# First attention's rotation sums, sums of squares, power and query planes moved from the projection into a stage of their own behind the scores

## The chip, the core and the metric

The kernel runs on one core of one Trainium2 chip. The time is the device time of one launch in microseconds; a version's figure is the median of several runs. Engines are named as the profile names them: PE (TensorE matmuls), PEld (TensorE weight loads), DVE (VectorE), ACT (ScalarE), POOL (GpSimd), SP (SyncE, which issues the DMAs).

## What is computed

Two transformer layers, each attention and then a feed-forward part, on an input of 4 sequences x 256 positions x 256 features in f32. Only the first attention is touched. Per sequence, with 16 query heads, 8 key/value heads and head size 128:

```python
q = einsum('btd,ndh->btnh', x, q_kernel);  k, v = einsum('bsd,ckdh->cbskh', x, kv_kernel)
q = apply_rope(rms_norm(q, q_norm_scale)); k = apply_rope(rms_norm(k, k_norm_scale))
mask = (j <= i) & (i - j < 128)
probs = softmax(where(mask, (q * ATTN_SCALE) @ k, min))
x = x + einsum('btnh,nhd->btd', probs @ v, out_kernel)        # x was layer-normed before q, k, v
```

The first feed-forward part (with a 2-of-4 sparsification), the second attention and the second feed-forward part (with a Hadamard transform) follow.

## The kernel before, in words

The first attention is a software pipeline (`pipelined`, L301) over 16 units: n = 4b+g is sequence b with head group g (4 query heads, 2 key/value heads). Six stages are called with lags 0, 1, 2, 3, 4, 4 in steps. In one step the code calls them in the order project, join, split, score, turn, attend, each for its own unit. A scheduler in the language's layer then orders the instructions of each engine from this; `tc.issue_after(x)` holds an instruction behind x in that order. Every engine runs its queue in the order it was given.

- **project** (`project0`, L409): for both row halves t, PE multiplies the normed x by the q weights (4 heads) and the k,v weights (L426, tiles pj). DVE multiplies each result by the sine and the cosine table (L431, tiles qs and qc), ACT squares it (L436, sq) and copies v out (L438). Then, still in project: DVE adds the two rotated parts (L443, the *rotation sum*, 128x768) and reduces the squares per head (L444, the *sum of squares*, ss). For n >= 6 POOL splits the queries into two 16-bit planes (L242 through `copy_gpsimd`, tile qpl), which SP transposes by DMA (L454, qplT). POOL then makes the inverse root by a power (L457, L460, L463, tile r) and scales the keys with it (L466).
- **turn** (`turn0`, L472), one step later: queries come to qT from the DMA's planes (DVE, L486), or for n < 6 through PE transposes (L481) and a DVE copy (L482); keys go through PE transposes (L492, tr_k) and an ACT copy to kT (L493).
- **score** (`probabilities`, L192), two steps behind project: four score tiles on PE (L204, L205), for each two masked copies with row maxima on DVE (L207, mx), the bias on DVE (L214, nb), exponentials on ACT (L217), reciprocals on DVE (L222, rs), normalization on POOL (L225).
- **split, join, attend**: POOL splits p into planes (L242, tile pl), SP transposes them (L251, plT), ACT joins them (L262, pT), PE multiplies with v (L380, L384, tile av), ACT copies av out (L388, zT). In the last units PE transposes p instead.
- **out** (L391): behind steps 8, 9, 12 and 13 one block of the output projection (L294, tile po).

PSUM has eight banks here: four of the tag `bank` (scores, av, po, early tr_k) and four of the tag `half` (pj, tr_q, and tr_k for 6 <= n < 14). A tile's bank is free for the next tile of its tag when its readers are done: scores by L207 on DVE, pj by L431 on DVE with L436 and L438 on ACT, av by ACT. The squares have two buffers, one for each t.

Of the kernel before, what the change touches and what calls it, by code (L numbers as in the profile page):

```python
# [20 lines left out]
F32 = mybir.dt.float32  # L21
# [3 lines left out]
ALU = mybir.AluOpType  # L25
AX = mybir.AxisListType

P = 128
B, T, D = 4, 256, 256
NT = T // P  # L30
# [18 lines left out]
def two_layers(ctx, tc, consts, tables, x, wq, wkv, wo, w_gate, w_up, w_down,  # L49
               w_k, w_q, w_v, w_o, w1, w3, w2, out):  # L50
    nc = tc.nc
# [92 lines left out]
    last_of = {}  # L144
# [171 lines left out]
    def attention0():  # L316
        with tc.tile_pool(name="attn0", bufs=2, reuse_waits="tile", side="right") as own:
            xnT, factors = {0: normed(0)}, {}


            cos_s = own.tile([P, NT, 2, HD], F32, name="cos_s", bufs=1)
            sin_s = own.tile([P, NT, 2, HD], F32, name="sin_s", bufs=1)
            with tc.issue_after(last_of["norm"].ins):
                for t in range(NT):
                    for tab, at in ((cos_s, 0), (sin_s, 256)):
                        src = angles[:, at + t * HD : at + (t + 1) * HD]
                        nc.vector.tensor_tensor(
                            tab[:, t], src.unsqueeze(1).to_broadcast([P, 2, HD]), scl, ALU.mult
                        )

            def project(n, _):
                b, g = divmod(n, 4)
                held = project0(own, xnT[b], g, cos_s, sin_s, n >= 6)
                if g == 1 and b + 1 < B:
                    factors[b + 1] = moments(b + 1)
                if g == 2 and b + 1 < B:
                    with tc.issue_after(last_of["qc"].ins):
                        xnT[b + 1] = normed(b + 1, factors[b + 1])
                return held

            def turn(n, held):
                rot, qT_planes, v, r = held
                return *turn0(own, rot, qT_planes, half if 6 <= n < 14 else bank), v, r

            def score(n, held):
                qT, kT, v, r = held
                ps = [
                    probabilities(
                        qT, kT, (2 * kk, 2 * kk + 1), mask0,
                        r[:, :, 2 * kk : 2 * kk + 2].rearrange("p t h -> p h t"),  # L350
                    )
                    for kk in range(2)
                ]
                return ps, v

            def split(n, held):
                ps, v = held
                return ps if n >= B * 4 - 3 else [
                    planes(p, own_planes) for p in ps
                ], v  # L360

            def own_planes(shape, name):
                return own.tile(shape, U16, tag="pl", name=name, bufs=4)

            def join(n, held):
                ps, v = held
                return [
                    transposed(ps[kk]) if n >= B * 4 - 3 else joined(ps[kk], ((
                        (nc.scalar.copy, slice(0, 2), last_of["exp"]),
                        (nc.scalar.copy, slice(0, 2), last_of["exp"]),  # L370
                    )[kk],)) for kk in range(2)
                ], v

            def attend(n, held):
                pTs, v = held
                zT = page("zT")
                for kk in range(2):
                    pT = pTs[kk]
                    av = bank([2, T], "av")
                    nc.tensor.matmul(  # L380
                        av, lhsT=v[:, 0, kk, :], rhs=pT[:, :, 0:T], start=True, stop=False,
                        skip_group_check=True,
                    )
                    nc.tensor.matmul(  # L384
                        av[:, :, P:T], lhsT=v[:, 1, kk, :], rhs=pT[:, :, T:],
                        start=False, stop=True, skip_group_check=True,
                    )
                    nc.scalar.copy(zT[:, 2 * kk : 2 * kk + 2, :], av)  # L388
                return zT

            def out(b, t, kept=False):  # L391
                def emit(done):
                    zTs = [done[4 * b + g] for g in range(4)]
                    if not kept:
                        project_out(bank([D], "po"), zTs, wo_sb, b, t)
                    else:
                        with tc.issue_after(last_of[0].ins):
                            project_out(half([D], "po"), zTs, wo_sb, b, t)
                return emit

            behind = {
                8: [out(0, 0)], 9: [out(0, 1)], 12: [out(1, 0)], 13: [out(1, 1)],
                17: [lambda _: xn_f.append(normed(0))],
                19: [lambda _: xn_f.append(normed(1)),
                     out(2, 0, True), out(2, 1, True), out(3, 0), out(3, 1)],
            }
            pipelined((project, turn, score, split, join, attend), (0, 1, 2, 3, 4, 4), behind, (0, 4, 3, 2, 1, 5))

    def project0(own, xnT, g, cos_s, sin_s, by_dma):  # L409


        v = own.tile([P, NT, 2, HD], F32, tag="v", name="v", bufs=5)
        r = small.tile([P, NT, 6], F32, tag="r", name="r")
        ss = small.tile([P, NT, 6], F32, tag="ss", name="ss")
        rot = []
        for t in range(NT):
            cols = slice(t * P, (t + 1) * P)
            sq = own.tile([P, 6, HD], F32, tag="sq", name="sq", bufs=2)
            qc = own.tile([P, 6, HD], F32, tag="qc", name="qc", bufs=4)
            qs = own.tile([P, 6, HD], F32, tag="qs", name="qs")  # L420

            for w, hs in ((wq_sb, slice(0, 4)), (wkv_sb, slice(4, 6))):
                pj = half([4, HD], "pj")
                n = hs.stop - hs.start
                for c in range(NC):
                    last_of[0] = nc.tensor.matmul(  # L426
                        pj, lhsT=xnT[:, c, cols], rhs=w[:, g, c, :],
                        start=(c == 0), stop=(c == NC - 1),
                    )
                for rot_to, tab in ((qs, sin_s), (qc, cos_s)):  # L430
                    last_of["qc"] = nc.vector.tensor_tensor(  # L431
                        rot_to[:, hs], pj[:, 0:n],
                        tab[:, t, hs.start // 4, :].unsqueeze(1).to_broadcast([P, n, HD]),
                        ALU.mult,
                    )
                nc.scalar.activation(sq[:, hs], pj[:, 0:n], AF.Square)  # L436
                if n == 2:
                    last_of["v", t] = nc.scalar.copy(v[:, t, :, :], pj[:, 2:4])  # L438
            rot.append((qc, qs, sq))
        for t, (qc, qs, sq) in enumerate(rot):  # L440

            parts = [i.rearrange("p n (s h) -> p n s h", s=2) for i in (qc, qs)]
            nc.vector.tensor_tensor(parts[0], parts[0], parts[1][:, :, ::-1, :], ALU.add)  # L443
            nc.vector.tensor_reduce(ss[:, t, :], sq, AX.X, ALU.add)  # L444
            rot[t] = qc
        qT_planes = None
        if by_dma:

            planes = page_of_planes([P, NT, 2, 4 * HD], "qpl")
            for t, qc in enumerate(rot):  # L450
                words = qc[:, 0:4, :].rearrange("p j h -> p (j h)").bitcast(U16)
                copy_gpsimd(planes[:, t], words.rearrange("p (n w) -> p w n", w=2))
            qT_planes = page_of_planes([P, NT * 2 * 4, P], "qplT")
            nc.sync.dma_start_transpose(qT_planes, planes.rearrange("p t w n -> p (t w n)"))  # L454

        ve = small.tile([P, NT, 6], F32, tag="ve", name="ve")
        nc.gpsimd.tensor_scalar(  # L457
            ve[:, :, 0:4], ss[:, :, 0:4], 1.0, HD * RMS_EPS, ALU.mult, ALU.add
        )
        nc.gpsimd.tensor_scalar(  # L460
            ve[:, :, 4:6], ss[:, :, 4:6], 1.0 / HD, RMS_EPS, ALU.mult, ALU.add
        )
        nc.gpsimd.tensor_tensor(r.rearrange("p t h -> p (t h)"), ve.rearrange("p t h -> p (t h)"),  # L463
                                mhalf, ALU.pow)
        for t, qc in enumerate(rot):
            last_of["k"] = nc.gpsimd.tensor_tensor(  # L466
                qc[:, 4:6, :], qc[:, 4:6, :],
                r[:, t, 4:6].unsqueeze(2).to_broadcast([P, 2, HD]), ALU.mult,
            )
        return rot, qT_planes, v, r  # L470

    def turn0(own, rot, qT_planes, bank_of_k):  # L472

# [474 lines left out]
```

## Time and profile before

| | |
|---|---|
| median of 3 runs | 755.07 us (754.88 to 755.31) |
| the profiled execution | 755.64 us, its span 753.8 us |
| granted TensorE clock | 1.000 |
| first attention | about 7 to 265 us of the span |
| busy, whole span | PE 98%, DVE 61%, ACT 53%, POOL 44% |

The profile is of one execution. An engine's busy time is the union of its instructions. Ends of matmuls are modelled, and each has a tail behind the time in which the next may start; so stalls of PE are best read from start to start: 0.430 us between two matmuls of 512 columns, 0.215 for 256, 0.109 for 128 when nothing is waited for.

### The profile page before, as it was taken

To read this page: it belongs to the slowest core of one execution; us is meant where nothing else is said; L and a number is where in the kernel's file an instruction comes from. 1 tells how busy PE (TensorE), PEld (TensorE's weight loads), DVE (VectorE), ACT (ScalarE), POOL (GpSimd) and SP (SyncE) were. 2 spreads that over 40 slices of the span, in tenths; PEclk is the share of its full clock that TensorE was granted. 3 is DMA by queue.
4 is the path that set the end of the run, shared out by engine and by line. 5 is a ranking of instruction groups with operands and counts; after the bars stand their busy time and mean duration, and the time that the engine had idled before them with its cause. 6 is when DMAs were issued, how large, how long until landed. Compare 5 with 4: busy or idle time off the path is not lost. (4 is left out here: it accounts for less than half of the span.)

```text
span 753.8 us, 11642 instructions
## 1 busy us (share of the span) xinstructions
PE 738.6 (98%) x3980; PEld 601.4 (80%) x3980; DVE 462.1 (61%) x1396; ACT 399.7 (53%) x985; POOL 330.0 (44%) x475
## 2 busy tenths in 40 slices
PE   8999999999999999999999999999999999999998
PEld 5556556656666788888899999999998899899997
DVE  6999886698678426987655644464443447344433
ACT  2378886678668722222346555555555675415332
POOL 1589998779678301011116433343338644220000
PEclk9999999999999999999999999999999999999999
DMA  8725445435433060001334422432232222002100
GB/s 322 284 42 71 69 86 100 82 59 108 73 70 71 1 223 14 16 15 22 119 70 84 127 43 43 98 100 43 43 71 43 43 43 42 2 0 22 27 10 28
DMA packets 121610, 53.30 MB, mean 71 GB/s; under 512 B 114768, under 2 KB 116944, under 8 KB 120784
## 3 DMA queue, kind: packets, MB, share of 16 engines
q1 hardware_dynamic: 121552, 52.57, 30.6%
q8 instruction: 31, 0.51, 0.3%
q14 instruction: 27, 0.22, 0.1%
HBM read 22.94 MB, written 1.05 MB: 32 GB/s over the span
## 5 line engine op out<-in xcount | busy, mean ns | idle before, releaser
L225 POOL TENSOR_SCALAR p<-p,rs 128x128 f32<-128x128 f32 (+1 forms) x256 | 120.9, 491 | 156.7 <-DVE rs L222 153.4
L207 DVE CUSTOM_DVE_ANT_0 p<-sc,cst 128x128 f32<-128x128 f32 (+1 forms) x256 | 78.7, 350 | 10.4 <-PE sc L205 7.8
L242 POOL TENSOR_SCALAR pl<-p 128x1536 uint16<-128x1536 uint16 x54 | 81.9, 1516 | 6.3 <-DMA plT<-pl 2.1
L262 ACT COPY pT<-plT 128x768 uint16<-128x768 uint16 (+1 forms) x54 | 77.1, 1486 | 1.8 <-DMA plT<-pl 1.8
L217 ACT ACTIVATE p<-p,nb,r 128x128 f32<-128x128 f32 (+1 forms) x128 | 68.2, 534 | 17.6 <-DVE nb L214 17.6
L426 PE MATMUL pj<-wq,xnT 128*128 128x512 f32 x128 | 61.8, 596 | 1.3 <-ACT xnT L179 0.7
L426 PE MATMUL pj<-wkv,xnT 128*128 128x512 f32 x128 | 60.9, 593 | 0.5 <-DMA wkv<-in_wkv_dram 0.5
L217 ACT ACTIVATE p<-p,nb 128x128 f32<-128x128 f32 (+1 forms) x128 | 56.3, 446 | 7.3 <-DVE nb L212 7.3
L282 PE MATMUL po<-w_o,zT 128*128 128x256 f32 x256 | 57.7, 379 | 0.0
L155 POOL TENSOR_SCALAR ve<-mv 128x2 f32<-128x2 f32 x16 | 3.4, 215 | 122.9 <-DVE mv L152 122.6
L294 PE MATMUL po<-wo,zT 128*128 128x256 f32 x256 | 57.2, 379 | 0.0
L294 PEld LDWEIGHTS po<-wo,zT 128*128 128x128 f32 x256 | 48.2, 190 | 6.3
L282 PEld LDWEIGHTS po<-w_o,zT 128*128 128x128 f32 x256 | 47.5, 190 | 5.8
L436 ACT ACTIVATE sq<-pj 128x512 f32<-128x512 f32 x64 | 29.6, 490 | 32.9 <-DVE qc L431 28.4
L426 PEld LDWEIGHTS pj<-wkv,xnT 128*128 128x128 f32 x128 | 23.8, 190 | 27.8 <-issue 24.4
L426 PEld LDWEIGHTS pj<-wq,xnT 128*128 128x128 f32 x128 | 23.0, 190 | 22.0 <-issue 17.8
L270 PE MATMUL av<-pT,v 128*128 128x256 f32 x128 | 38.9, 386 | 1.4 <-DVE mx L207 1.2
L222 DVE RECIPROCAL rs<-sm 128x4 f32<-128x4 f32 x64 | 11.2, 176 | 46.7 <-ACT p L217 46.1
L205 PE MATMUL sc<-kT,qT 128*128 128x256 f32 x128 | 38.2, 381 | 0.1
L205 PE MATMUL sc<-qk 128*128 128x256 f32 x128 | 38.2, 380 | 0.0
L632 ACT COPY qk<-qk_x 128x512 f32<-128x512 f32 x16 | 9.4, 586 | 53.8 <-PE qk_x L741 50.4
L463 POOL TENSOR_TENSOR r<-ve,mhalf 128x12 f32<-128x12 f32 x16 | 37.3, 2331 | 1.3
(154 smaller groups left out, 1773.3 us busy)
## 6 DMA issues: line engine op xcount, KB each, us to landing
w<-in_w_dram SPq DMA_DIRECT2D x3, 1024.0 KB, 4.8
wq<-in_wq_dram SPq DMA_DIRECT2D x4, 512.0 KB, 7.7
wkv<-in_wkv_dram SPq DMA_DIRECT2D x4, 512.0 KB, 8.0
wo<-in_wo_dram SPq DMA_DIRECT2D x4, 512.0 KB, 10.2
w_qk<-in_w_q_dram SPq DMA_DIRECT2D x4, 512.0 KB, 5.1
w_qk<-in_w_k_dram SPq DMA_DIRECT2D x4, 512.0 KB, 6.0
w_v<-in_w_v_dram SPq DMA_DIRECT2D x4, 512.0 KB, 7.2
w_o<-in_w_o_dram SPq DMA_DIRECT2D x4, 512.0 KB, 6.3
```

The lines of the kernel that those rows point to most:

```text
L205: nc.tensor.matmul(sc[:, P : 3 * P], lhsT=q[:, P:T], rhs=k, start=True, stop=True)
L207: last_of["mx"] = nc.vector.tensor_tensor_reduce(out=p[:, j, cols], in0=sc[:, cols], in1=mask[:, cols], scale=1.0, scalar=-3.0e38, op0=ALU ...
L217: last_of["exp"] = nc.scalar.activation(p[:, j, cols], p[:, j, cols], AF.Exp, bias=nb[:, j, i : i + 1], scale=SCALE1 if rq is None else rq ...
L225: nc.gpsimd.tensor_scalar(p[:, j, cols], p[:, j, cols], rs[:, j, i : i + 1], 1.0, ALU.mult, ALU.mult)
L242: nc.gpsimd.tensor_scalar(o, i, 1.0, 1.0, ALU.mult, ALU.mult)
L262: copy(words.rearrange("p (n w) -> p w n", w=2), halves[:, :, js].rearrange("p w j n -> p w (j n)"),)
L270: nc.tensor.matmul(av, lhsT=v0, rhs=pT[:, 0:T], start=True, stop=False, skip_group_check=True)
L282: nc.tensor.matmul(po[:, t, :], lhsT=zT[:, j, t * P : (t + 1) * P], rhs=w[:, j, :], start=(t == j == 0), stop=(j == 3), skip_group_check=True,
L294: nc.tensor.matmul(po, lhsT=zTs[hd // 4][:, hd % 4, t * P : (t + 1) * P], rhs=w[:, hd, :], start=(hd == 0), stop=(hd == n - 1),)
L426: last_of[0] = nc.tensor.matmul(pj, lhsT=xnT[:, c, cols], rhs=w[:, g, c, :], start=(c == 0), stop=(c == NC - 1),)
L436: nc.scalar.activation(sq[:, hs], pj[:, 0:n], AF.Square)
L463: nc.gpsimd.tensor_tensor(r.rearrange("p t h -> p (t h)"), ve.rearrange("p t h -> p (t h)"), mhalf, ALU.pow)
```

## The change

The tail of `project0` becomes a function `rotate0` and a stage `rotate` with lag 0, called behind score and ahead of turn. For units 2 to 13 the rotation sum is also held behind the last row maximum of the score of the same step (`first`). Operations, tiles and buffer counts stay.

```diff
-                held = project0(own, xnT[b], g, cos_s, sin_s, n >= 6)
+                held = project0(own, xnT[b], g, cos_s, sin_s)
...
+            def rotate(n, held):
+                rot, v = held
+                rot, qT_planes, r = rotate0(rot, n >= 6, last_of["mx"] if 2 <= n < 14 else None)
+                return rot, qT_planes, v, r
...
-            pipelined((project, turn, score, split, join, attend), (0, 1, 2, 3, 4, 4), behind, (0, 4, 3, 2, 1, 5))
+            pipelined(
+                (project, rotate, turn, score, split, join, attend), (0, 0, 1, 2, 3, 4, 4),
+                behind, (0, 5, 4, 3, 1, 2, 6),
+            )
...
+        return rot, v
+
+    def rotate0(rot, by_dma, first):
+
+        r = small.tile([P, NT, 6], F32, tag="r", name="r")
+        ss = small.tile([P, NT, 6], F32, tag="ss", name="ss")
         for t, (qc, qs, sq) in enumerate(rot):
 
             parts = [i.rearrange("p n (s h) -> p n s h", s=2) for i in (qc, qs)]
-            nc.vector.tensor_tensor(parts[0], parts[0], parts[1][:, :, ::-1, :], ALU.add)
+            with tc.issue_after(first.ins) if first else nullcontext():
+                nc.vector.tensor_tensor(parts[0], parts[0], parts[1][:, :, ::-1, :], ALU.add)
             nc.vector.tensor_reduce(ss[:, t, :], sq, AX.X, ALU.add)
...
-        return rot, qT_planes, v, r
+        return rot, qT_planes, r
```

The body of `rotate0` behind the sums (query planes, their DMA transpose, L457 to L466) is that of `project0`, unchanged. How the scheduler orders the built program of each version on each engine is used in the prediction.

## The prediction

> **What bounds the kernel.** I read the page's busy shares first, then busy time by stretches, then PE's timeline, then the queues of DVE and POOL around its largest stall. The shares and three stretches (columns: PE, PEld, DVE, ACT, POOL, clock, DMA):
>
> ```profile
> PE 738.6 (98%) x3980; PEld 601.4 (80%) x3980; DVE 462.1 (61%) x1396; ACT 399.7 (53%) x985; POOL 330.0 (44%) x475
> ```
>
> ```profile
> 50.00:100.00 50.00, 49.19 (x191) 29.31 (x190) 46.45 (x136) 44.13 (x108) 48.07 (x64) 1.00 0.46 72
> ...
> 150.00:200.00 50.00, 47.99 (x180) 30.12 (x179) 42.13 (x115) 36.29 (x87) 40.09 (x52) 1.00 0.46 81
> ...
> 450.00:500.00 50.00, 50.00 (x325) 46.37 (x324) 26.33 (x96) 27.67 (x80) 17.03 (x25) 1.00 0.32 75
> ```
>
> PE sets the end everywhere. In the second attention (450 to 500) nothing else is near; in the first, four engines are: 46 to 49 us of 50 for DVE, POOL and PE. There a late neighbour stalls PE, and an order decides who is late. PE's work is untouched, so only its stalls can be won. Its timeline, rows with idle time in the brackets:
>
> ```profile
> 43.81 0.71 PE L204 MATMUL sc<-kT,qT 128*128 128x128 f32 x4 [1.00 <-ACT kT L493]
> ...
> 102.25 1.12 PE L380 MATMUL av<-pT,v 128*128 128x512 f32 x2 [1.00 <-DVE mx L207]
> ...
> 115.98 1.12 PE L380 MATMUL av<-pT,v 128*128 128x512 f32 x2 [0.47 <-DVE mx L207]
> ...
> 169.66 1.13 PE L380 MATMUL av<-pT,v 128*128 128x512 f32 x2 [1.46 <-DVE mx L207]
> ```
>
> From start to start, with the 0.1 us by which the matmul after a stall is late too, the stalls between 30 and 190 us are: 0.48 at 35.7, 1.26 at 43.8, 0.31 at 61.6, 0.69 at 83.5, 0.41 at 87.3, 1.27 at 102.3, 0.49 at 114.4, 0.74 at 116.0, 1.72 at 169.7 and 0.81 at 183.0. Together 8.2 us: the stock the change can draw on. After 230 us another 2 us lie in the drain, where project has ended. Why av waits at 169.66 shows in DVE's timeline:
>
> ```profile
> 166.29 0.28 DVE L207 CUSTOM_DVE_ANT_0 p<-sc,cst 128x128 f32<-128x128 f32 x1
> ...
> 166.49 1.91 DVE L443 TENSOR_TENSOR qc<-qc,qs 128x768 f32<-128x768 f32 x1
> 168.33 0.94 DVE L444 TENSOR_REDUCE ss<-sq 128x6 f32<-128x768 f32 x1
> 169.19 0.41 DVE L207 CUSTOM_DVE_ANT_0 p<-sc,cst 128x256 f32<-128x256 f32 x1
> ```
>
> A rotation sum and a sum of squares stand between the first and second row maximum. They free no PSUM bank; the maxima behind them do, and av needs the first score's bank. POOL meanwhile, and the line that says it waits for the sums:
>
> ```profile
> 166.13 1.47 POOL L242 TENSOR_SCALAR pl<-p 128x1536 uint16<-128x1536 uint16 x1
> 168.49 1.05 POOL L242 TENSOR_SCALAR qpl<-qc 128x1024 uint16<-128x1024 uint16 x1 [0.89 <-DVE qc L443]
> 169.61 0.20 POOL L457 TENSOR_SCALAR ve<-ss 128x8 f32<-128x8 f32 x1
> 169.88 0.20 POOL L460 TENSOR_SCALAR ve<-ss 128x4 f32<-128x4 f32 x1
> 170.16 2.52 POOL L463 TENSOR_TENSOR r<-ve,mhalf 128x12 f32<-128x12 f32 x1
> 172.75 1.19 POOL L466 TENSOR_TENSOR qc<-qc,r 128x256 f32<-128x256 f32 x2
> ```
>
> ```profile
> POOL qpl L242 <- DVE qc L443: 17.9, 9, 2.8
> ...
> DVE ss L444 <- ACT sq L436: 2.2, 3, 0.9
> ```
>
> Keys of that step are scaled by 173.9; PE transposes them at 181.0. This slack of 7 us is what the change spends.
>
> **The change, part by part.** [...]PE durations per step, start to start: scores 2.6, key transposes 0.44, av 2.6, project 6.9, an output block 6.9; so 12.5 us without and 19.4 with a block. I call T the start of a step's scores on PE.
>
> *DVE.* In the built order of after, a steady step reads: products of project (3.75 us), eight maxima with one bias among them (2.5), rotation sum, bias, rotation sum, reciprocal, sum of squares, two query copies (0.67 each), reciprocal. One sum of squares usually stays inside project's products. The 1.9 to 3.0 us from the first maximum's start to the second's, at 98.8, 113.1, 166.3 and 180.6, shrink to 0.2. The price: the second bias stands behind the first rotation sum (0.95), covered while ACT works 2.1 us on the first head pair's exponentials; query copies and the next project's products stand about 3 us later.
>
> *PE.* The order also moves: before, one projection matmul instruction (0.86) stood between key transposes and av; now av follows at once and needs its bank at T+3.0, and project comes whole behind.
>
> Laid out step by step with these durations, the early part: layer-norm's xn no longer stands behind two sums, so 0.48 at 35.7 goes; 5.2 us more of project stand between tr_k and the next scores, so kT is in time and 1.26 at 43.8 goes. But the bank of the query transposes (PE path, n < 6) is freed by a copy that now stands behind both rotation sums: maxima done at T+3.5, sums and bias to 5.6, reciprocal, copy done at 6.5 in step 2, where PE wants the bank at 5.6; with the restart 1.0. In step 3, where PE also has both sets of transposes first, it lacks 0.6. New stalls 1.0 + 0.6; without cover by the projection they would be the whole 2 to 3 us. The 0.31, 0.69 and 0.41 go: their waits were on DVE's and ACT's turn behind the same sums.
>
> Steps 7 and 8 (unit 7): the first maximum still waits, because the sum of squares kept in project waits for ACT's squares, which stand behind a joining copy of 1.9 us (the waits line above has the like, 0.9 long). I get maxima from T+2.8 and a stall of 0.45 at av, in place of 1.27. The 0.49, 0.74, 1.72 and 0.81 go.
>
> *POOL,* where the debt falls due. Before: planes, power and key scaling ran in their own step, ahead of normalization. After: query planes (2 x 1.05), normalization of one head pair (1.7), L457 and L460 (0.55), pl (1.5), normalization of the other pair (1.7), power (2.35), key scaling (2 x 0.6). In step 7 the maxima end at T+5.1, the first rotation sum at 6.1; POOL, idle for some 3 us, starts its planes at 6.2 and, with all of this behind it, has the two halves of the keys scaled at 16.7 and 17.3. PE comes to their transposes one step later: 12.9+2.6 = T+15.5. They end 1.65 late with the restart. In step 11 the maxima end at T+3.8; the same chain gives 15.4 and 16.0 against 15.1, so 0.75. In step 3, without planes, scaling ends at T+14.6, just in time. Behind an output block (6.9 us more) it is never late, nor for units 6, 10 and 14, whose two sums of squares are in time for the power to be issued earlier.
>
> Here a rule speaks against the change. The Trainium skill, "SBUF — State Buffer", section "Who interferes with whom": a DVE instruction with two SBUF inputs and a GpSimd instruction reading SBUF hold the shared read interface in turn, the second fully blocked. The row above agrees: the rotation sum, 0.95 us elsewhere (at 99.0, 113.3, 180.8), took 1.91 with pl from 166.13 to 167.60. After, the second sum comes due just as the first releases the query planes on POOL. Had I let them overlap, as my sum so far does, the debt would be 1.65 + 0.75; taken in turn, whoever is first, planes end 1.0 later and both stalls grow by that: 2.65 + 1.75. I take the latter, since the row shows it; its lower bound is none of it.
>
> *SP.* The order of its queue is unchanged. The query transpose waits for its planes, now some 5 us later, but on POOL the next pl stands behind those planes as well, so no plT waits newly. It took 1.94 us and its data are read a step later: no price while a step's 12 us cover it; without that, 2 us.
>
> **Sum.** Away: 8.2. New: 1.0 + 0.6 + 0.45 + 2.65 + 1.75 = 6.45. Net -1.75 us. The drain after 230 us changes order slightly (rotation sums of units 14 and 15 aren't held behind maxima); I leave it at zero, between a gain of 2 and a loss of 2, its present stalls. Of the profiled execution 755.64 - 1.75 = 753.9 (span 752.05); it stood 0.57 above the median, so 753.3.
>
> **The rivals.** *The keys' power is later still (slower).* Place: POOL between rotation sum and key scaling, in steps 3, 7, 11. If the sums meet normalization or pl instead of an idle POOL, or ACT's exponentials hold up the reciprocal, the chain slips further. Each us costs PE one us at units 7 and 11, and at unit 3 beyond 0.5. It decides from 1.3 us of further delay: 3.4 more stall, slower by over 1.5. At 2 us: 2+2+1.5 = 5.5, net +3.75: 758.8. For it: POOL 48.1 of 50 busy. Against: POOL's own sum per step is 12.4, and PE's full 12.5 or 19.4.
>
> *The stall only changes its name.* DVE, ACT and POOL have about 12.4 us of work for 12.5 of PE, so non-output steps may stay at the 13.7 to 14.3 us seen before, and only about half of the early gains remain: some 0.3 us net, 754.8. For it: ss waits for ACT's squares before and after. Against: sums behind the maxima are DVE work that can lag without holding a bank.
>
> *Keys are in time after all.* If POOL catches up within its step, the 4.4 us of key stalls drop out: 8.2 - 2.05 = 6.15 us won, 749.0. For it: my chain puts every POOL wait in series. Against: power stands behind two normalizations in the built order.
>
> **Numbers.** Likeliest, 753.3 with its own range 751.5 to 754.6: 0.42. Keys in time, 749.0: 0.17. Changed name, 754.8: 0.18. Later power, 758.8: 0.23. 0.2% of 755.07 is 1.5 us, about what a measurement of this kernel can tell from no change. Faster: 0.33 of the likeliest and all of 0.17, 0.50. Same: 0.09 and the 0.18, 0.27. Slower: 0.23. Some 0.08 lies below 749.0 and 0.12 above 758.0, which gives the range; it covers the rule's 2 us and the drain's 2.
>
> **What would show it.** Right: DVE's maxima run eight in a row, followed by both rotation sums; no av in the non-output steps stalls over 0.6; tr_k of units 7 and 11 waits on POOL's L466 for 1 to 3 us; the second rotation sum or the first qpl takes 1.8 to 2.0. Wrong: stalls at tr_k in most steps, or scores waiting for kT or for av banks because zT comes late on ACT (then the power rival or a wait that I haven't costed); or PE stalls in the drain above 4 us. If the stalls named above went and the time did not fall, the sum of new ones is mis-sized.

## The result and the profile after

The changed kernel takes 764.77 us (median of 4 runs, 763.93 to 764.91); the kernel before took 755.12 beside it (754.88 to 755.31). The ratio is 1.0126, with an interval of 1.0111 to 1.0141: 1.3% slower. The profiled execution took 764.65 us, its span is 762.9, 9.1 us longer than before. In the changed kernel the rotation sum is L456, the sum of squares L457, the power L476, the key scaling L479, the key transposes L505, av L385 and L389; L207, L214, L225 and L242 keep their numbers.

The page's shares, and two stretches of the changed kernel (columns as before: PE, PEld, DVE, ACT, POOL, clock, DMA):

```profile
PE 742.3 (97%) x3980; PEld 604.0 (79%) x3980; DVE 463.7 (61%) x1396; ACT 400.4 (52%) x985; POOL 333.5 (44%) x475
```

```profile
100.00:150.00 50.00, 46.62 (x168) 30.46 (x169) 33.56 (x97) 32.98 (x79) 39.06 (x48) 0.97 0.43 79
150.00:200.00 50.00, 46.21 (x164) 28.85 (x163) 38.06 (x107) 36.09 (x85) 44.40 (x55) 0.93 0.43 80
```

Between 150 and 200 us PE ran 164 matmul instructions, where before ran 180 in the same stretch, and the clock column, 1.00 all through before, shows 0.97 and 0.93. So two things were lost: time in which PE waits, and speed. PE's timeline of the changed kernel shows both, at unit 7's keys and at unit 11's:

```profile
114.79 0.44 PE L505 MATMUL tr_k<-cst,qc 128*128 128x128 f32 x2 [2.53 <-POOL qc L479]
116.07 0.44 PE L505 MATMUL tr_k<-cst,qc 128*128 128x128 f32 x2 [0.85 <-POOL qc L479]
...
118.27 1.91 PE L385 MATMUL av<-pT,v 128*128 128x512 f32 x2
...
185.43 0.69 PE L505 MATMUL tr_k<-cst,qc 128*128 128x128 f32 x2 [2.79 <-POOL qc L479]
186.79 0.69 PE L505 MATMUL tr_k<-cst,qc 128*128 128x128 f32 x2 [0.67 <-POOL qc L479]
187.27 1.91 PE L385 MATMUL av<-pT,v 128*128 128x512 f32 x2
```

The key transposes wait for the key scaling on POOL. Start to start, the stalls are 2.69 and 1.01 us at unit 7, 2.96 and 0.98 at unit 11. After them the same pair of av matmuls that takes 1.02 us elsewhere takes 1.91: two matmuls of 512 columns start 0.85 apart instead of 0.43. The granted clock of just these stretches confirms it:

```profile
116.40:120.60 4.20, 4.20 (x10) 2.21 (x9) 3.31 (x5) 4.20 (x16) 4.20 (x3) 0.59 0.30 57
...
187.20:192.20 5.00, 5.00 (x10) 2.64 (x9) 2.97 (x3) 3.46 (x6) 5.00 (x6) 0.51 0.43 79
```

PE counts as fully busy in both, but at a mean clock of 0.59 and 0.51; in the 8 to 9 us behind each the clock is 1.00 again. (The stretches are cut by hand. The clock itself reads 0.50 from 116.99 to 120.40 and from 185.25 to 192.08; the last section shows that.) Summed over the matmul starts, the slow stretches cost 1.69 us at unit 7 and 2.65 at unit 11 (0.32 of it in the transposes themselves, 0.69 a pair where the others take 0.44).

All of before's stalls of 30 to 190 us that waited for maxima are gone, and the waits of the changed kernel between 30 and 230 us have other names (columns: us in total, times, longest). For av behind DVE's maxima the same list shows 1.0 us in two waits, where before had 3.5 in four.

```profile
POOL qpl L242 <- DVE nb L214: 22.0, 5, 9.3
...
PE tr_k L505 <- POOL qc L479: 6.8, 4, 2.8
```

DVE, at the end of unit 7's step, does what was built: maxima in a row (the first of the eight starts at 99.23), then both rotation sums with a bias between them.

```profile
101.52 0.95 DVE L456 TENSOR_TENSOR qc<-qc,qs 128x768 f32<-128x768 f32 x1
102.39 0.16 DVE L214 SCALAR_TENSOR_TENSOR nb<-mx,r 128x4 f32<-128x4 f32 x1
102.47 0.95 DVE L456 TENSOR_TENSOR qc<-qc,qs 128x768 f32<-128x768 f32 x1
```

POOL's queue from there, in the changed kernel (left out are the two short instructions on the sums of squares):

```profile
102.57 3.89 POOL L242 TENSOR_SCALAR qpl<-qc 128x1024 uint16<-128x1024 uint16 x2 [3.10 <-DVE nb L214]
106.44 1.64 POOL L225 TENSOR_SCALAR p<-p,rs 128x128 f32<-128x128 f32 x4
...
108.70 1.47 POOL L242 TENSOR_SCALAR pl<-p 128x1536 uint16<-128x1536 uint16 x1
110.16 1.64 POOL L225 TENSOR_SCALAR p<-p,rs 128x128 f32<-128x128 f32 x4
111.76 2.28 POOL L476 TENSOR_TENSOR r<-ve,mhalf 128x12 f32<-128x12 f32 x1
114.12 1.90 POOL L479 TENSOR_TENSOR qc<-qc,r 128x256 f32<-128x256 f32 x2
```

This is the predicted chain, item by item. POOL is idle for 3.1 us, then planes, a normalization, pl, the other normalization, the power, the key scaling: PE wanted the keys at 112.1 and had the second half at 116.0. Two rows are longer than the same work before: two planes take 3.89 us (2 x 1.05 before), the scaling 1.90 (1.19 before; its halves are 0.61 and 1.33).

### The profile page after: what moved, and what is told of

Its sections match the earlier page's. It is cut to its first block, busy times and chain, and to the rows that moved or that the text cites. A ratio compares the mean times of both kernels' runs of the same rounds, so it can differ in the third digit from the quotient of the medians.

```text
span 762.9 us, 11658 instructions
## 1 busy us (share of the span) xinstructions
PE 742.3 (97%) x3980; PEld 604.0 (79%) x3980; DVE 463.7 (61%) x1396; ACT 400.4 (52%) x985; POOL 333.5 (44%) x475
## 3 DMA queue, kind: packets, MB, share of 16 engines
HBM read 22.94 MB, written 1.05 MB: 31 GB/s over the span
## 5 line engine op out<-in xcount | busy, mean ns | idle before, releaser
L225 POOL TENSOR_SCALAR p<-p,rs 128x128 f32<-128x128 f32 (+1 forms) x256 | 116.6, 473 | 158.3 <-DVE rs L222 154.7
L207 DVE CUSTOM_DVE_ANT_0 p<-sc,cst 128x128 f32<-128x128 f32 (+1 forms) x256 | 79.1, 352 | 11.1 <-PE sc L205 7.9
L242 POOL TENSOR_SCALAR pl<-p 128x1536 uint16<-128x1536 uint16 x54 | 80.3, 1486 | 3.6
L432 PEld LDWEIGHTS pj<-wq,xnT 128*128 128x128 f32 x128 | 23.5, 190 | 26.0 <-issue 19.5
L437 DVE TENSOR_TENSOR qs<-pj,sin_s 128x512 f32<-128x512 f32 x64 | 35.2, 550 | 10.0 <-PE pj L432 9.6
L242 POOL TENSOR_SCALAR qpl<-qc 128x1024 uint16<-128x1024 uint16 x20 | 28.1, 1418 | 24.8 <-DVE nb L214 24.8
## 6 DMA issues: line engine op xcount, KB each, us to landing
wo<-in_wo_dram SPq DMA_DIRECT2D x4, 512.0 KB, 10.3
```

Of the source, the lines that this page charges most:

```text
L207: last_of["mx"] = nc.vector.tensor_tensor_reduce(out=p[:, j, cols], in0=sc[:, cols], in1=mask[:, cols], scale=1.0, scalar=-3.0e38, op0=ALU ...
L225: nc.gpsimd.tensor_scalar(p[:, j, cols], p[:, j, cols], rs[:, j, i : i + 1], 1.0, ALU.mult, ALU.mult)
L242: nc.gpsimd.tensor_scalar(o, i, 1.0, 1.0, ALU.mult, ALU.mult)
L432: last_of[0] = nc.tensor.matmul(pj, lhsT=xnT[:, c, cols], rhs=w[:, g, c, :], start=(c == 0), stop=(c == NC - 1),)
```

## The experiments

The theory after the result: the 9.1 us come from one place in POOL's queue, key scaling behind two normalizations in the steps of units 7 and 11, and PE's half clock after each of the two waits adds 4.3 us to their 7.6. Rivals: the loss is spread, sums on DVE behind the maxima cost in every step; or it is the hold behind the maxima; or the half clock has a cause of its own.

**1. Units 7 and 11 as before, the rest as in the change**

```diff
                 held = project0(own, xnT[b], g, cos_s, sin_s)
+                if n in (7, 11):
+                    rot, qT_planes, r = rotate0(held[0], n >= 6, None)
+                    held = rot, qT_planes, held[1], r
...
             def rotate(n, held):
+                if n in (7, 11):
+                    return held
```

> Units 7 and 11 are rotated inside project again, all others as in the change. Theory K (the keys' scaling of units 7 and 11 comes late on POOL, PE waits 3.7 and 4.3 us for it and then runs at half clock for 1.7 and 2.3 us; 12.0 us in all): these 12 us go, the two av stalls of before in these steps (1.3 and 1.7) return: 764.7 - 12.0 + 3.0 = 755.7, clock 1.00. Rival D (the loss is spread over all steps by DVE's hold of the sums behind the maxima: later query copies, biases and products): two units of fourteen give back little, 761 or more.

Measured: 751.69 us (751.47 to 753.52), ratio to before 0.9962 [0.9948, 0.9977]. Two of sixteen units carry more than the whole loss: 13.1 us less than the change. PE has no stall above 0.15 us from 85 to 149 us; before's av stalls in these steps did not come back, since the scheduler now has two projection instructions between key transposes and av there. The loss is not spread. In the drain unit 15's keys still wait, 1.30 and 0.75 us. The profiled execution (753.52) runs at half clock behind them and has a mean clock of 0.998; the other three, at 1.000, took 751.5 to 751.8.

**2. The power made cheap**: the inverse root by an addition, so the factors of the norm are not computed in this kernel; order and shapes stay.

```diff
         nc.gpsimd.tensor_tensor(r.rearrange("p t h -> p (t h)"), ve.rearrange("p t h -> p (t h)"),
-                                mhalf, ALU.pow)
+                                mhalf, ALU.add)
```

> The power on POOL (2.28 us) is replaced by an addition of the same operands (some 0.2 us), so the norm factors aren't computed; all else as in the change. Theory K: POOL's chain to the keys is 2.1 us shorter, the first waits fall from 2.7 and 3.0 to 0.6 and 0.9, too short for the clock to fall: 2.1 + 1.7 and 2.1 + 2.3 off, some 1 us in the drain: 764.7 - 9 = 755.5 (754 to 758), clock 1.00. If POOL's chain is not on the path: within 1 us of 764.7.

Measured: 750.54 us (750.32 to 750.57), ratio 0.9940 [0.9926, 0.9953]. POOL's timeline of this kernel at unit 7, then PE's:

```profile
108.51 1.63 POOL L225 TENSOR_SCALAR p<-p,rs 128x128 f32<-128x128 f32 x4
110.10 0.21 POOL L476 TENSOR_TENSOR r<-ve,mhalf 128x12 f32<-128x12 f32 x1
110.39 1.18 POOL L479 TENSOR_TENSOR qc<-qc,r 128x256 f32<-128x256 f32 x2
```

```profile
111.06 1.01 PE L505 MATMUL tr_k<-cst,qc 128*128 128x128 f32 x4 [0.26 <-POOL qc L479]
```

Taking 2.07 us off one POOL instruction of each unit took 14.2 us off the kernel; more than the 12.0 of units 7 and 11, since the av stall at 72.5 and the drain's waits for unit 15's keys are gone too. The wait shrinks from 3.70 to 0.72 at unit 7 and from 3.94 to 0.30 at unit 11, more than the power's own 2.07 each time: with the power short, the key scaling is over before the next step's rotation sums start on DVE, and takes 1.18 instead of 1.90. No half clock is left.

**3. The same edit on the kernel before**, again without the norm factors, as a control: in case the power is simply on the path of any version.

> Control on the kernel before: the same cheap addition in place of the power, so the norm factors aren't computed. There keys were ready 7 us ahead of their transposes. Theory K: POOL's power isn't on the path before, so 754 to 755.5, and what the cheap power took off the change (14 us) was the change's own debt. If the power costs in both kernels alike, 745 or less.

Measured: 754.86 us (754.24 to 755.23), ratio 0.9999 [0.9991, 1.0008], with the power at 0.21 us. Before, the power as a whole costs nothing; the change put it on the path. Single stalls do move in this trace (1.02 and 0.31 us at 73.4 and 1.74 at 88.5 are new, others are smaller), and their sum stays.

**4. Keys ahead of normalization, in the steps of units 7 and 11 only.** The normalization L225 of those steps is kept in a list (`late`) and issued behind the last key scaling. PE's, DVE's, ACT's and SP's orders are those of the change; on POOL, the two normalizations move behind the scaling, and with them one pl.

```diff
+            def normal(n, held):
+                hold = n + 2 in (7, 11) and n + 2 < B * 4
+                with tc.issue_after(last_of["k"].ins) if hold else nullcontext():
+                    for fn in late:
+                        fn()
+                late.clear()
+                return held
...
-                (project, rotate, turn, score, split, join, attend), (0, 0, 1, 2, 3, 4, 4),
-                behind, (0, 5, 4, 3, 1, 2, 6),
+                (project, rotate, turn, score, normal, split, join, attend),
+                (0, 0, 1, 2, 2, 3, 4, 4), behind, (0, 6, 5, 3, 1, 4, 2, 7),
```

> The change as it is, but in steps 7 and 11 alone POOL's two normalizations and their planes are issued behind the key scaling. The orders of DVE, PE, ACT and SP are those of the change, instruction for instruction. Theory K: both waits of PE and the half clock go, 12.0 us; the drain keeps its stalls and may fall to half clock there, as it did in two runs (2 us): 752.7 (751.5 to 755). Rival D (loss from DVE's hold): 762 or more, as no sum has moved. Earlier all steps were treated so and gave 756.5: if that was the cost of late normalization as such, and not of the first steps, then 755 to 757 here too.

Measured: 754.48 us (753.31 to 756.45, 13 runs), ratio 1.0000 [0.9992, 1.0008], 10.3 us less than the change. POOL, then PE, of this kernel at unit 7 (here the scaling is L495, the key transposes L521):

```profile
107.22 2.28 POOL L492 TENSOR_TENSOR r<-ve,mhalf 128x12 f32<-128x12 f32 x1
109.58 1.19 POOL L495 TENSOR_TENSOR qc<-qc,r 128x256 f32<-128x256 f32 x2
110.75 3.24 POOL L226 TENSOR_SCALAR p<-p,rs 128x128 f32<-128x128 f32 x8
113.95 2.92 POOL L247 TENSOR_SCALAR pl<-p 128x1536 uint16<-128x1536 uint16 x2
```

```profile
112.52 0.60 PE L521 MATMUL tr_k<-cst,qc 128*128 128x128 f32 x4
...
117.28 5.02 PE L299 MATMUL po<-wo,zT 128*128 128x256 f32 x22 [1.33 <-DVE mx L207]
```

The key scaling ends at 110.8, ahead of PE, the scaling is back to 1.19, and both waits and both slow stretches (12.0 us in the change) are gone. So the place in POOL's queue is the cause. A new wait of 1.49 us start to start has come, at the output block, and DVE's timeline of this kernel names its reason, one the prediction had no step for:

```profile
113.73 3.15 DVE L214 SCALAR_TENSOR_TENSOR nb<-mx,r 128x4 f32<-128x4 f32 x1
```

A bias of four elements a partition, 0.16 us elsewhere, takes 3.15, and ends with the second of two pl in a row (113.95 + 2.92 = 116.87). The last maxima stand behind it and hold the banks.

**5. Keys ahead of normalization in every step**: as the last one, with the hold for all units. Here DVE's and ACT's orders differ from the change's in a few places too.

> The change as it is, but POOL's normalizations of a step are issued behind the key scaling of the same step. DVE's order, hold included, stays. Theory K: the waits at the key transposes go, with the half clock after them: 764.7 - 12.0 = 752.7 (751 to 754.5), below before. Rival D: nothing in DVE's order has changed, so 761 or more. A third outcome: normalization, now 5 us later, makes planes and av late: new waits at av, 756 to 760.

Measured: 756.46 us (754.35 to 756.93, 11 runs), ratio 1.0014 [1.0005, 1.0023]: the third outcome. The waits at units 7 and 11 are gone here too, but unit 5's step (the profiled execution, 755.12) has the stretched bias again, and pays for it:

```profile
71.45 1.93 DVE L214 SCALAR_TENSOR_TENSOR nb<-mx,r 128x4 f32<-128x4 f32 x1
```

```profile
73.77 2.07 PE L400 MATMUL av<-pT,v 128*128 128x512 f32 x2 [1.80 <-DVE mx L207]
```

Here two pl end at 73.36, the bias at 73.38; av waits 1.96 us start to start (1.00 in the change) and then runs at half clock for 3.4 us. Keys ahead of normalization gain at units 7 and 11, where the keys are late, and lose at unit 5, where they are not.

**6. PE kept busy while it waits**: 12 and 4 matmuls of the identity into free columns of the same bank, ahead of the two pairs of key transposes of units 7 and 11. The waits stay, only the idleness goes.

```diff
-            tk = bank_of_k([2, P], "tr_k")
+            tk = bank_of_k([4, P], "tr_k")
+            for i in range(fill[t]):
+                nc.tensor.matmul(
+                    tk[:, 2 + i % 2, :], lhsT=ident, rhs=ident, start=True, stop=True
+                )
...
-            nc.scalar.copy(kT[:, :, cols], tk)
+            nc.scalar.copy(kT[:, :, cols], tk[:, 0:2])
```

> The change with extra work: before the key transposes of units 7 and 11 PE multiplies the identity with itself 12 times ahead of the first half and 4 times ahead of the second (2.6 and 0.87 us), into unused columns of the same PSUM tile, in the time in which it waits. If the half clock after the waits is a consequence of PE standing still: clock 1.00 and 1.7 + 2.3 us off, less up to 0.4 by which the filler outlasts a wait: 760.5 to 761.5. If the lower clock has another cause (load on the chip, the run), the time stays at 764 to 765 and the clock at 0.993.

Measured: 759.37 us (758.67 to 760.45), ratio 1.0060 [1.0045, 1.0075], 5.4 us less than the change. PE's timeline and the clock of the stretch behind the first wait:

```profile
112.38 2.84 PE L506 MATMUL tr_k<-cst 128*128 128x128 f32 x24
115.06 0.38 PE L510 MATMUL tr_k<-cst,qc 128*128 128x128 f32 x2
115.28 1.06 PE L506 MATMUL tr_k<-cst 128*128 128x128 f32 x8
...
116.46 1.02 PE L386 MATMUL av<-pT,v 128*128 128x512 f32 x2
```

```profile
116.40:120.60 4.20, 4.20 (x18) 2.96 (x17) 3.94 (x6) 4.20 (x11) 4.20 (x3) 1.00 0.29 54
```

av starts at 116.46, as in the change (116.35): the keys are as late as ever. But the clock stays at 1.00 and the pair takes 1.02. So the slow stretches come from PE's idleness, and they were worth 1.69 + 2.65 = 4.34 us by the change's trace. By the starts of the same matmuls, this execution is 0.3 us behind the change's when unit 7's step begins, gains 4.5 at the two places, loses 1.7 in the drain, where its matmuls run at half clock, and gains 1.6 behind 600 us, in work that the change doesn't touch; together the 4.2 by which its span (758.7) is shorter. Of its four runs the two at a mean clock of 1.000 took 758.7 and 758.8, the two at 0.998 760.0 and 760.5. The rest of the loss is the waits.

**7. No hold behind the maxima**: the new stage stays, `first` is None for all units.

```diff
-                rot, qT_planes, r = rotate0(rot, n >= 6, last_of["mx"] if 2 <= n < 14 else None)
+                rot, qT_planes, r = rotate0(rot, n >= 6, None)
```

> The stage stays where the change put it, but no rotation sum is held behind the maxima; the scheduler then puts the first half's sum ahead of the maxima and the second behind them, and on POOL the power behind one normalization, not two. Theory K: keys of units 7 and 11 come 2.5 to 3 us earlier, in time or within 1 us; no half clock: 764.7 - 10 = 754 to 755.5. If the place of the stage alone, not the hold, makes the keys late: 762 or more.

Measured: 755.84 us (755.00 to 757.50, 12 runs), ratio 1.0017 [1.0008, 1.0025]. Neither unit 7 nor unit 11 waits (the scheduler puts the power ahead of the second normalization), so the hold is the part that made the keys late. The stage alone gains nothing: other stalls come, 0.82 at 46.4, 1.93 at 52.1 (projection behind a query copy), 0.97 at 88.8, and the drain's.

**8 to 10. Which units may be late.** As experiment 1, with other lists of units in project, one line each for experiments 8, 9 and 10:

```diff
-                if n in (7, 11):
+                if n in (7, 11, 14, 15):
+                if n in (2, 3, 4, 5, 7, 11, 14, 15):
+                if n in (3, 4, 5, 7, 11, 14, 15):
```

> As the run with units 7 and 11 rotated inside project, and 14 and 15 so too. That run kept stalls in the drain: scores of unit 14 0.95, key transposes of unit 15 waiting for POOL 2.0, then half clock 1.7; of before's order there I know 0.6, 0.4 and 0.3. Theory K: 751.7 - 4.6 + 1.3 = 748.4 (747 to 750). If the drain's end is set by something else (the last softmax chain), 751 to 752.

Measured: 750.76 us (750.49 to 751.15), ratio 0.9944 [0.9931, 0.9956]; the drain's stalls fall to 0.78 and less. That is 2.4 us above the 748.4 expected; 1.7 of it is the half clock in the drain of experiment 1's profiled execution, which the sum took off a median that did not contain it.

> As the run before it in this call, and units 2 to 5 rotated inside project as well, so the late stage is left to units 6, 8, 9, 10, 12 and 13. It prices the early steps. From the trace of the change: 0.48, 1.26 and 0.31 of before went there, 0.36, 1.07 and 1.00 came: near zero, so 748 to 749. If late rotation gains at units 2 to 5, slower by 1 or more than the run with them late; if it costs there, faster by 1 or more.

Measured: 750.74 us (750.65 to 751.12), ratio 0.9943 [0.9927, 0.9958]. Equal to the last: early on, the change trades before's stalls (0.48 at 35.7, 1.16 at 43.9, 0.31, 0.58, all back in this trace) against its own of the same sum. What a late rotation can win lies in the steps of units 6, 8, 9, 10, 12 and 13; with units 7 and 11 out of it, PE's stretch from 150 to 200 us reads:

```profile
150.00:200.00 50.00, 50.00 (x194) 32.60 (x193) 44.82 (x129) 38.80 (x98) 43.90 (x52) 1.00 0.43 80
```

PE is never idle there (47.99 of 50 before), and busy for 49.67 of the 50 ahead of it (48.30 before). Experiments 8 and 9 are the fastest versions, 4.3 us ahead of before.

> Search for a better version: the late stage for units 2, 6, 8, 9, 10, 12 and 13, all others rotated inside project. Unit 2 late took away stalls of 0.48 and 1.26 and brought 0.36; units 3 to 5 late brought 1.07 and 1.00 for 0.31 and 0.4. If these add up: 750.7 - 1.4 = 749.3. If they are coupled: 750.7.

Measured: 751.52 us (750.97 to 751.71), ratio 0.9954 [0.9941, 0.9966]. A miss: unit 2 late saves the two stalls at 35.7 and 43.9, but 0.36 and 0.59 at the projection (39.1, 51.0), 1.06 and 0.31 at the key transposes at 74.2 and 0.55 at 85.9 come in their place.

## Why the prediction was wrong

The sum of stalls, from start to start, by the prediction's own terms and as the changed kernel's trace has them (the first row counts the 0.1 us by which the matmul behind a stall is late too, the measured new ones do not):

| term | predicted, us | measured, us |
|---|---|---|
| stalls of before, 30 to 190 us | -8.2 | -8.2 |
| query-transposes' bank, steps 2 and 3 (38.6, 50.5) | 1.0 + 0.6 | 0.36 + 1.07 |
| av of step 7 (99.9) | 0.45 | 0.35 |
| keys of unit 7, wait | 2.65 | 2.69 + 1.01 = 3.70 |
| keys of unit 11, wait | 1.75 | 2.96 + 0.98 = 3.94 |
| half clock behind the two waits | not in the sum | 1.69 + 2.65 = 4.34 |
| av at 72.5 | not in the sum | 1.00 |
| two small ones (84.4, 154.7) | not in the sum | 0.26 + 0.49 |
| drain, against before | 0 (within 2) | +1.7 |
| sum | -1.75 | +9.0 (spans: +9.1) |

**The step that failed** is the POOL step, where the prediction put the debt of the keys at "2.65 + 1.75". Its mechanism, its place (units 7 and 11, nowhere else in the steady part) and what it rests on (power behind two normalizations) were right: experiments 1, 2 and 4 each remove it and with it 13.1, 14.2 and 10.3 us. The two terms were mis-sized, 4.4 us where 7.6 were measured, and a consequence, the half clock, was put at nothing without a reason, where 4.3 were measured. Between the sum predicted and the sum measured lie 10.8 us: 3.2 from the mis-sized waits, 4.3 from the half clock, 1.7 from the drain and 1.75 from three stalls that stood in no sum, less 0.3 by which two terms came out smaller.

*The waits, 7.6 us instead of 4.4.* PE came when predicted: unit 7's step starts at 96.5 and PE wants the keys 15.6 later (predicted 15.5); unit 11's at 167.3, wanted 15.2 later (15.1). The keys came 19.5 and 19.4 us into the step where 18.3 and 17.0 were predicted. At unit 7 the planes took 3.89 for two, 0.8 more than 2 x 1.05 + 1.0, and the key scaling 0.7 more than 1.2. At unit 11 the planes began half a us later than in the working (the first rotation sum met a pl and took 1.53 us, from 171.05), a normalization took 2.06 instead of 1.7, and the scaling took 2.69:

```profile
172.75 3.21 POOL L242 TENSOR_SCALAR qpl<-qc 128x1024 uint16<-128x1024 uint16 x2 [0.96 <-DVE nb L214]
175.94 2.06 POOL L225 TENSOR_SCALAR p<-p,rs 128x128 f32<-128x128 f32 x4
...
184.04 2.69 POOL L479 TENSOR_TENSOR qc<-qc,r 128x256 f32<-128x256 f32 x2
```

DVE of the same kernel in that moment:

```profile
183.94 0.96 DVE L456 TENSOR_TENSOR qc<-qc,qs 128x768 f32<-128x768 f32 x1
...
185.31 0.95 DVE L456 TENSOR_TENSOR qc<-qc,qs 128x768 f32<-128x768 f32 x1
```

The late key scaling runs into the rotation sums of the next step, and each of its halves takes 1.33 and 1.40 us instead of 0.61. The prediction applied the Trainium skill's rule ("SBUF — State Buffer", "Who interferes with whom": DVE with two SBUF inputs and GpSimd take the shared read interface in turn) at the head of the chain only. It holds at its end as well, and there lateness makes more lateness: once the power ends past the next step's maxima, the scaling pays 0.7 to 1.5 us more. Experiment 2 shows the reverse: 2.07 us off the power, 3.0 and 3.6 off the waits. At the head the working left out DVE's two query copies, which run beside the planes and the first normalization (1.29 us from 104.26, 2.13 from 174.38). That they account for the longer planes at unit 7 and the longer normalization at unit 11 is read from these times; no run took them away.

*The half clock, 4.3 us, was in no case.* The profile of before shows 1.000 everywhere, with no wait above 1.7 us in the steady part, so nothing in it priced a wait of 3 us. The Trainium skill, "TensorE: Matmul & The Clock Gate", Part 1, does: half rate after an idle window of about 3.4 us, by a window that runs freely. The traces here agree on the window and differ on how idle it has to be: in none was PE idle throughout, and 1.7 to 2.6 us were enough (last section). The prediction's own 2.65 plus its range would have been reason enough to weigh it. Experiment 6 shows the term alone.

*The 1.00 at 72.5*, against "no av in the non-output steps stalls over 0.6", is the stretched bias. DVE and POOL of the changed kernel:

```profile
71.06 1.05 DVE L214 SCALAR_TENSOR_TENSOR nb<-mx,r 128x4 f32<-128x4 f32 x1
```

```profile
70.63 1.47 POOL L242 TENSOR_SCALAR pl<-p 128x1536 uint16<-128x1536 uint16 x1
```

The bias (two SBUF inputs, the maxima and r) ends at 72.11, pl at 72.10. The prediction had costed the rotation sum against pl, not the 0.16 us bias, which stands ahead of maxima that free banks. That the interface is what holds it is read from the coinciding ends, here and in experiments 4 and 5, and from unit 7's step, where POOL is idle and the same bias (at 100.55) takes 0.16; no kernel was run that differs in this alone.

*The drain* stayed within its bound of 2 us, but not at zero: unit 15's keys wait 1.31 and 0.74, and a score 1.06 for a query copy. Experiment 8, which puts units 14 and 15 back, takes most of it away.

**What was right.** The eight maxima in a row; all 8.2 us of stalls gone; 1.43 instead of 1.6 at the query transposes' bank; 0.35 instead of 0.45 at av; and no cost on SP. The early steps are not among this: up to 87.3 us the prediction had 3.15 us going and 1.6 coming, a gain of 1.5, but experiment 9 against 8 shows none (750.74 and 750.76), since 1.00 at 72.5 and 0.26 at 84.4 come on top.

**The rivals.** "The keys' power is later still (slower)" is what happened: the keys were 1.2 us later still at unit 7 and 2.4 at unit 11, where it named 1.3 as its turning point. That made the waits 3.2 us longer, by its own count (3.4) no more than the edge of slower; the half clock and the stalls outside the sum made the rest. It gave 758.8 at 2 us, with 1.5 at unit 3, where nothing waits, and nothing for the clock. Of its two reasons, sums meeting POOL's work was the true one, though most of that meeting is at the chain's end. "The stall only changes its name" and "keys in time after all" are out; the latter is about what experiments 8 and 9 reach (750.75 against 749.0).

## What to carry to other kernels

When an operation is moved back on DVE, write out the queue of the engine behind it to the last consumer, and check every instruction of that chain, not only the first, against what the other engine runs at its new time: two-input DVE work and POOL work stretch each other. PE waits that come to 2 to 4 us in one place must be priced with what can follow them, here 1.7 to 2.7 us lost to half-speed matmuls, so waits close together cost far more than the same sum spread out. And where a move loses, look first whether it loses in all steps or in few: here 2 units of 16 held the loss, and with these and the last two put back the rest of the move was worth 4.3 us.

## What the runs showed of the hardware that was not expected

- PE's clock halved after waits that no row of before had, and it changed only at points a whole number of 3.41 us apart. In the changed kernel it falls at 116.99, rises at 120.40, falls at 185.25 and rises at 192.08: 3.41, 64.85 (19 x 3.41) and 6.83 us (2 x 3.41). Windows of the changed kernel along these points:

```profile
113.57:116.98 3.41, 1.35 (x6) 0.87 (x7) 3.33 (x9) 1.72 (x6) 3.33 (x4) 1.00 0.01 2
116.99:120.40 3.41, 3.41 (x6) 1.69 (x5) 2.60 (x4) 3.41 (x14) 3.41 (x3) 0.50 0.30 57
...
181.84:185.25 3.41, 0.80 (x5) 0.39 (x3) 3.41 (x19) 2.66 (x9) 3.33 (x2) 1.00 0.48 87
185.26:188.66 3.40, 2.56 (x6) 1.45 (x7) 3.40 (x6) 3.37 (x13) 3.40 (x4) 0.50 0.00 0
188.67:192.08 3.41, 3.41 (x7) 1.78 (x6) 1.50 (x3) 1.99 (x2) 3.41 (x5) 0.50 0.62 115
...
250.11:253.52 3.41, 2.05 (x9) 1.29 (x10) 2.54 (x8) 3.41 (x11) 3.33 (x7) 1.00 0.00 0
```

  Before the two falls PE was idle for 2.06 and 2.61 us of the window (its 3.41 less PE's busy time, whose ends are modelled), before that of experiment 5 for 1.97. The clock came back after windows with 0.00 us idle (0.17 in experiment 5), and not after the one from 185.26, with 0.84.
- The length of the wait does not decide alone; its place in this raster goes with the outcome. In the drain, the same pair of waits (1.30 to 1.31, then 0.74 us) was followed by slow matmuls in experiments 1 and 6 and by none in the changed kernel. PE's timelines of the changed kernel, then of experiment 1, and a window of experiment 1:

```profile
250.89 0.44 PE L505 MATMUL tr_k<-cst,qc 128*128 128x128 f32 x2 [1.14 <-POOL qc L479]
...
252.18 1.02 PE L385 MATMUL av<-pT,v 128*128 128x512 f32 x2
```

```profile
238.32 0.44 PE L510 MATMUL tr_k<-cst,qc 128*128 128x128 f32 x2 [1.13 <-POOL qc L484]
...
239.64 1.92 PE L390 MATMUL av<-pT,v 128*128 128x512 f32 x2
```

```profile
236.17:239.58 3.41, 1.70 (x10) 1.03 (x9) 3.30 (x16) 3.41 (x7) 3.33 (x4) 1.00 0.00 0
```

  Experiment 1 has both waits in one window, with 1.71 us idle, and the clock falls at its end, 239.59; experiment 6 likewise (1.72, fall at 248.25). In the changed kernel the point at 250.11 cuts the first wait, and 1.36 us are left in the window behind it.

  The raster lies differently in each execution: counted from the start of the span in steps of 3.41 us, its points are 0.93 us off in the changed kernel, and 0.65, 1.91 and 2.49 in experiments 1, 5 and 6. The Trainium skill's page named above says as much, that the window runs freely. How much idleness it takes is not sharp in these profiles: windows with 1.71 us idle in experiment 4 (from 238.49) and 1.77 in experiment 7 (from 49.48) had no fall, on rasters worked out from where the clock first rises. No run moved a wait along the raster on purpose. It fits that one kernel runs with or without a fall: in experiment 7 the seven runs at a mean clock of 1.000 took 755.0 to 756.0 us, the five at 0.998 757.0 to 757.5. In experiments 4 and 5 clock and time do not part so cleanly, and the rest of their spread stays open.
- An instruction of 0.16 us can hold an engine for 3.15 us, if it falls due while the other engine runs two long ones in a row (experiment 4).
